# An index bound on the experts' gathers and additions, and the sort put first in the opening stage

## The chip, the cores and the metric

The kernel runs on one core of one Trainium2 chip. The metric is the device time of one execution in microseconds; the median of three runs is used. Lower is better.

## The reference

Four residual layers work on x, 2048 tokens (4 batches of 512) of 512 numbers each, all in float32:

1. Each token belongs, by its id, to one of four context matrices c (512 x 512), and takes tanh(g) times silu(h cᵀ) * (h cᵀ) times c, with h the layer-normalized token. In the kernel, "experts" of this stage are the four context matrices.
2. A gated feed-forward layer of width 2048, whose activations and weights are rounded to a small float format in blocks of 32.
3. Attention of eight heads over the channels, with queries from x and keys and values from the context.
4. A mixture of 64 experts (width 192, six per token, chosen in groups). An expert takes at most CAP = 96 tokens; further ones are dropped:

```
flat_e = topk_ids.reshape(-1)
order = argsort(flat_e);  se = flat_e[order]
pos = arange(Tn * K) - searchsorted(se, se, side='left')
valid = pos < CAP                      # CAP = 96
buf = zeros(E, CAP + 1, H).at[se, slot].set(x[tok])[:, :CAP]
h = silu(buf @ w_gate) * (buf @ w_up)
out = h @ w_down                       # weighted and added to each token's row
y + silu(x @ ws_gate) * (x @ ws_up) @ ws_down     # one shared expert for all tokens
```

Slots of an expert that no token takes are zero rows in `buf`, and their results are not used.

## The kernel before

The program is one pass over the four layers. In the first stage an order written out by hand fixes the instruction order on TensorE, ScalarE, VectorE and GpSimd (`tc.manual_schedule(engines={PE, ACT, DVE, POOL})`); SyncE's queue (SP), which issues most DMAs, is ordered by the scheduler. In the second and third layer the order is fixed on TensorE, ScalarE and VectorE, and in the expert stage by the scheduler alone.

The first stage does three things side by side.

- Sorting. Token ids become a one-hot table (`hot`, L341), TensorE counts ranks and totals (`rank_ps` L348, `tot_ps` L350), VectorE sums the totals over tiles (`scan`, L354 to L359), works out each token's place (`pos`, `place`, L374 to L387), writes one-hot rows (`hot_tile` L391, `hot_row` L399), TensorE inverts the table (`at_ps`, L406), and VectorE makes `to_row` (L423) and `from_row` (L425). With them GpSimd gathers sorted tiles of x by indirect DMA (`take`, L442), NS = 19 tiles of 128 rows, eleven of them ahead.
- The context. Four loads `c_sb` (L307, two buffers) are transposed by `turn_context(b)`: four chunks of four transposes (L294) and a copy by ScalarE (L295) into `cT`.
- The second layer's weights. `quantize()` rounds 24 blocks of weights on VectorE (L245 to L268), in pieces; `some_weights(us)` does pieces worth so many microseconds, so that they lie between the other work. A block's source is loaded by SP (L196, L213) into one of four buffers; when a block's `w_q` (L263) is made, `fetch_weights(1)` issues the next load. ScalarE makes `mx_wide` (L251) for each block, and `turn_weights` transposes the result.

For each sorted tile `sums_of` takes two passes on ScalarE (L150), `factors_from` works out the layer norm's factors for a group of tiles on VectorE (`ln_mean`, L156 and on), `normal` normalizes (L170), and the loop over i turns the tile, multiplies it by its context matrix twice (L474) with `squashed` and `gated` (L486) between, and adds the rows to the table `x_rows` in DRAM by an indirect DMA (L491).

Before the loop, SP also issues copies and zeros: x to `x_rows` (L311), zeros to the spare rows of `x_rows`, `h_rows` and `out` (L312 to L314), to all of `more_rows` (L316, L317), and the list of unused slots to `taken` (L318). `zeros` is a tile that VectorE clears at L298.

In the third stage the router fills `taken`: for every slot of every expert it notes which token sits there (`noted`, through `put`, L123). A slot that nobody takes keeps its number from `unused`, which points at one of the 96 spare rows T to T+95, rows of zeros in `h_rows` and rows that nobody reads in `out` and `more_rows`. At the end of this stage the last token tiles go through `groups_of`, `experts_of`, `counted` (L1041), `slots` and `noted` one after another.

In the expert stage `gather(e)` fetches 96 rows of 576 numbers (512 of the token, 64 weights) through column e of `idx` into `xg` (L1194, six buffers, six experts ahead); `turn` transposes them (`g_ps`, L1207), `hidden` multiplies by the gate and up weights (`gu_ps`, L1217), `finish` by the down weights (`e_y`, L1240), copies to `e_o` (L1242, four buffers) and adds the 96 rows to a table by an indirect DMA (L1243). Even experts add to `out`, odd ones to `more_rows`, the last three to `out`. Additions to one table follow each other. Weights of an expert come by three DMAs on SP (`e_gu`, `e_gu`, `e_dn`), up to 15 experts ahead. At the end `more_rows` is read back as `rest` (L1278), the shared expert's product (`sh_y`, L1294) is added to it (L1296) and the sum is added to `out` by GpSimd's DMAs (L1297).

Of the kernel before, what the change touches and what calls it, by code (L numbers as in the profile page):

```python
# [9 lines left out]
F32 = mybir.dt.float32  # L10
# [9 lines left out]
P = 128  # L20
B, S, D = 4, 512, 512
T = B * S
# [24 lines left out]
def flamingo_kernel(  # L47
# [19 lines left out]
    out: bass.AP,  # L67
):
    nc = tc.nc
    PE, ACT, DVE, POOL = (getattr(mybir.EngineType, e) for e in ("PE", "Activation", "DVE", "Pool"))  # L70
# [112 lines left out]
    with (  # L183
# [3 lines left out]
        tc.tile_pool(name="c_rows", bufs=2) as cp,  # L187
        tc.tile_pool(name="ps_t", bufs=4, space=PSUM) as ps_t,
        tc.tile_pool(name="ps_m", bufs=4, space=PSUM) as ps_m,
        tc.manual_schedule(engines={PE, ACT, DVE, POOL}),  # L190
    ):

        def rows_of(w, wT, rb):
# [81 lines left out]
        def some_weights(us):  # L275

            while us > 0:
                took = next(weights, None)
                if took is None:
                    return  # L280
                us -= took
# [3 lines left out]
                turn, q = rounded.popleft()  # L285
                turn(q)

        def turn_context(b):

            c_sb = c_rows.popleft()  # L290
            for k in range(KC):
                ps = ps_t.tile([P, D], F32, name="cT_ps", tag="t")
                for s in range(4):
                    nc.tensor.transpose(ps[:, bass.ts(s, P)], c_sb[:, s, bass.ts(k, P)], ident)  # L294
                nc.scalar.copy(cT[:, b * KC + k, :], ps)  # L295
# [5 lines left out]
        with tc.tile_pool(name="route0", bufs=1) as rp:  # L301

            fetch_weights(1)
            c_rows = deque()
            for b in range(B):
                c_sb = cp.tile([P, 4, D], F32, name="c_sb")
                nc.sync.dma_start(c_sb, cx[bass.ts(b, S), :].rearrange("(j p) d -> p j d", p=P))  # L307
                c_rows.append(c_sb)
                if b == 1:
                    fetch_weights(3)  # L310
            nc.sync.dma_start(x_rows[:T, :], x[:, :])  # L311
            nc.sync.dma_start(x_rows[T:, :], zeros[:, :D])  # L312
            nc.sync.dma_start(h_rows[T:TP, :], zeros[:CAP, :])
            nc.sync.dma_start(out[T:TP, :], zeros[:CAP, :D])  # L314
            for j in range(NT):
                nc.sync.dma_start(more_rows[bass.ts(j, P), :], zeros[:, :D])  # L316
            nc.sync.dma_start(more_rows[T:TP, :], zeros[:CAP, :D])  # L317
            taken_by = [nc.sync.dma_start(taken[1 : CAP * E + 1, :].rearrange("(s e) o -> s (e o)", e=E), unused)]  # L318

            th = keep.tile([P, 4], F32, name="th")  # L320
            nc.scalar.activation(th, gains[:, 0:4], AF.Tanh)
# [26 lines left out]
            nc.tensor.matmul(rank_ps.rearrange("p j e -> p (j e)"), before, hot2, start=True, stop=True)  # L348
            tot_ps = ps_m.tile([P, NT, NE0], F32, name="tot_ps", tag="m")
            nc.tensor.matmul(tot_ps.rearrange("p j e -> p (j e)"), ones, hot2, start=True, stop=True)  # L350
            turn_context(0)
            some_weights(2.5)
            scan = [rp.tile([P, NT, NE0], F32, name=f"scan{i}") for i in range(2)]
            nc.vector.tensor_copy(scan[0], tot_ps)  # L354
            cur, step = 0, 1
# [41 lines left out]
            for j in range(0, NT, 4):  # L397
# [2 lines left out]
                    hot_row[:, j : j + 4], column.unsqueeze(1).to_broadcast(wide),  # L400
                    row_i[:, j : j + 4].unsqueeze(2).to_broadcast(wide), ALU.is_equal,
                )
            turn_context(1)
            at_ps = ps_m.tile([P, 2, NS], F32, name="at_ps", tag="m")
            for j in range(NT):
                nc.tensor.matmul(at_ps, hot_row[:, j, :], hot_tile[:, :, j, :], start=j == 0, stop=j == NT - 1)  # L406

            own = rp.tile([1, NS], F32, name="own")
            own1 = rp.tile([1, NS], F32, name="own1")
# [30 lines left out]
        def take(i):  # L440
            xs = wp.tile([P, D], F32, name="xs", bufs=XS)
            nc.gpsimd.indirect_dma_start(  # L442
                out=xs[:, :],
                out_offset=None,
                in_=x[:, :],
                in_offset=bass.IndirectOffsetOnAxis(ap=from_row[:, i : i + 1], axis=0),
            )
# [67 lines left out]

        for i in range(XS):
            take(i)
        turn_context(2)
        some_weights(4.0)
        turn_context(3)  # L520
        sums_of(0)
        some_weights(4.0)
        factors_from(0)
        sums_of(1)
        sums_of(2)
        normal(0)
        some_weights(4.0)
        factors_from(1)
        for i in range(3, 5):
# [2 lines left out]
        for i in range(-2, NS):  # L532
            if i >= 0:
                turned(i, "s", "sT")
            if i + 2 < NS:
                turned(i + 2, "h", "hT")
            waiting = len(rounded)
            if waiting:
                turn_weights()
            if i >= 0:  # L540
                times_context(i, "sT", "y")
            if 0 <= i + 1 < NS:
                squashed(i + 1)
            some_weights(3.6)
            if 0 <= i + 1 < NS:
                gated(i + 1)
            if i + 2 < NS:
                times_context(i + 2, "hT", "z")
            if waiting > 1:
                turn_weights()  # L550
            if i + 3 < NS:
                normal(i + 3)
            if i >= 0:
                add_rows(i)
                if i + XS < NS:
                    take(i + XS)
            sums_of(i + 7)
            some_weights(3.6)
            factors_from(i + 4)
        while rounded or sources:  # L560
# [617 lines left out]
    with (  # L1178
# [10 lines left out]
        tables = out, more_rows  # L1189
        LAST = 3  # L1190
        gathered = {}
        def gather(e):
# [42 lines left out]
        def finish(e, aT):  # L1235

            _, dn, held = loaded.pop(e)
            y = ps_m.tile([CAP, D], F32, name="e_y", tag="m")
            for c in range(2):
                nc.tensor.matmul(y, aT[:, c, :], dn[:, c, :], start=c == 0, stop=c == 1)  # L1240
            o = xp.tile([CAP, D], F32, name="e_o", bufs=4)
            nc.scalar.copy(o, y)  # L1242
            nc.gpsimd.indirect_dma_start(  # L1243
                out=tables[e % 2 if e < E - LAST else 0][:, :],
                out_offset=bass.IndirectOffsetOnAxis(ap=idx[:, e : e + 1], axis=0),
                in_=o[:, :],
                in_offset=None,
                compute_op=ALU.add,
            )
# [5 lines left out]
        AHEAD = 6  # L1255
# [71 lines left out]
```

## Time and profile before

| what | us |
|---|---|
| median of 3 runs | 1227.52 (1226.75 to 1229.18) |
| the profiled execution's own time | 1232.19 |
| its span | 1230.4 |
| TensorE busy | 1018.0 (83%) |
| VectorE busy | 792.9 (64%) |
| ScalarE busy | 572.3 (47%) |
| GpSimd busy | 385.4 (31%) |

The profile is of one execution. Its page gives the busy time of each engine, the span in 40 slices, the DMA queues, the chain of work that ended last, and groups of instructions by source line. The timeline lists instructions by start and length, with the idle time before them and what ended it in brackets. Times count from the start of the span. TensorE's matmul is PE, its weight load PEld, VectorE is DVE, ScalarE ACT, GpSimd POOL, SyncE SP; a q behind a name is that engine's queue issuing a DMA. The stages lie at about 0 to 251 us (first layer), 251 to 528 (second), 528 to 866 (third, with the router) and 866 to 1182 (experts), and the rest is the end.

### The profile page before, as it was taken

The numbers are of one execution on the slowest core, as the hardware profiler recorded it, in microseconds if no ns is written. First come the engines' busy times: TensorE is split into PE (matmuls) and PEld (weight loads), VectorE is DVE, ScalarE is ACT, GpSimd is POOL, SyncE is SP. The second block draws the span as 40 slices with busy tenths as digits, with TensorE's granted clock in tenths as the row PEclk, the third lists the DMA queues.
The fourth block names the chain that finished last, engine by engine and source line by source line (L and its number), as shares of the span: only waits on it lengthen the run. The fifth ranks groups of instructions, "written<-read, shape, count | busy, mean of one in ns | idle before, by whom it ended". The sixth has DMA issues, their size and how long they took to land. (4 is left out here: it accounts for less than half of the span.)

```text
span 1230.4 us, 14849 instructions
## 1 busy us (share of the span) xinstructions
PE 1018.0 (83%) x4603; PEld 512.5 (42%) x4603; DVE 792.9 (64%) x1976; ACT 572.3 (47%) x1144; POOL 385.4 (31%) x526
## 2 busy tenths in 40 slices
PE   5488998627888888788999999971899999999994
PEld 4244444313333334344454444440455555544441
DVE  7699999948998999846888887862222222222221
ACT  3665765437676657584665666630111111111120
POOL 3122322200000000011544544554355435444424
PEclk8698999958999999999999999985899999999997
DMA  9834543331221111187121111027799999999978
GB/s 333 320 86 103 109 97 77 51 112 35 43 50 28 18 18 18 18 229 218 55 70 55 56 61 46 22 76 222 230 272 273 279 280 284 276 282 279 277 186 137
DMA packets 75806, 174.76 MB, mean 142 GB/s; under 512 B 13024, under 2 KB 14064, under 8 KB 75664
## 3 DMA queue, kind: packets, MB, share of 16 engines
q1 hardware_dynamic: 51696, 128.04, 34.4%
q0 software_dynamic: 23200, 45.16, 19.2%
q8 instruction: 38, 0.62, 0.2%
q10 hardware_dynamic: 832, 0.62, 0.2%
q14 instruction: 40, 0.33, 0.1%
HBM read 133.76 MB, written 44.20 MB: 145 GB/s over the span
## 5 line engine op out<-in xcount | busy, mean ns | idle before, releaser
L1217 PE MATMUL gu_ps<-e_gu,gT 128*96 128x384 f32 x512 | 178.3, 491 | 0.0
L1221 DVE SCALAR_TENSOR_TENSOR a<-s,xg,gu_ps 96x192 f32<-96x192 f32 x64 | 35.0, 546 | 149.7 <-ACT s L1219 145.1
L1240 PE MATMUL e_y<-e_dn,eaT 96*96 96x512 f32 x256 | 120.5, 592 | 0.1
L123 POOL DMA_INDIRECT taken<-token_no,to_i x96 | 97.1, 1012 | 51.1 <-issue 24.2
L1217 PEld LDWEIGHTS gu_ps<-e_gu,gT 128*96 128x96 f32 x512 | 79.2, 165 | 62.5 <-issue 62.2
L631 ACT ACTIVATE p<-at_s,low 128x512 f32<-128x512 f32 x128 | 87.7, 697 | 28.6 <-DVE low L622 27.1
L1242 ACT COPY e_o<-e_y 96x512 f32<-96x512 f32 x64 | 37.3, 582 | 134.4 <-PE e_y L1240 57.2
L622 DVE TENSOR_REDUCE low<-at_s 128x2 f32<-128x1024 f32 x64 | 77.7, 1215 | 34.1 <-PE at_s L617 34.1
L1209 DVE COPY gT<-g_ps 128x384 f32<-128x384 f32 x64 | 35.7, 558 | 97.9 <-PE g_ps L1207 91.5
L747 POOL DMA_DIRECT2D x_rows<-y_sb x15 | 12.9, 863 | 262.1 <-ACT y_sb L746 262.1
L718 PE MATMUL gu<-wgT,hT 128*128 128x512 bf16 x256 | 72.0, 407 | 20.7 <-DVE inter L731 13.5
L491 POOL DMA_INDIRECT x_rows<-y_sb,to_row x19 | 39.5, 2081 | 150.3 <-ACT y_sb L490 150.3
L718 PEld LDWEIGHTS <-hT 128*128 128x128 bf16 x512 | 50.1, 103 | 86.3 <-DVE inter L731 14.3
L1243 POOL DMA_INDIRECT out_dram<-e_o,idx x34 | 48.8, 1435 | 117.3 <-ACT e_o L1242 51.8
L891 ACT COPY pT<-p_ps 128x512 f32<-128x512 f32 x128 | 70.9, 600 | 31.2 <-PE p_ps L890 30.5
L1194 POOL DMA_INDIRECT xg<-h_rows,idx x64 | 60.0, 938 | 62.3 <-DVE a L1221 24.2
L890 PE MATMUL p_ps<-ident,p 128*128 128x128 f32 x512 | 73.3, 281 | 7.3 <-ACT hT L968 6.7
L890 PEld LDWEIGHTS p_ps<-ident,p 128*128 128x128 f32 x512 | 54.5, 141 | 58.3 <-issue 22.7
L474 PE MATMUL l_mm<-cT,sT 128*128 x152 | 75.1, 641 | 0.0
L1219 ACT ACTIVATE s<-gu_ps 96x192 f32<-96x192 f32 x64 | 21.0, 328 | 116.2 <-PE gu_ps L1217 109.8
L617 PE MATMUL at_s<-c_tile,q 64*128 64x512 f32 x256 | 72.0, 640 | 1.3 <-ACT p L631 1.3
L474 PE MATMUL l_mm<-cT,hT 128*128 x152 | 71.4, 614 | 1.9 <-ACT hT L461 1.9
(245 smaller groups left out, 2022.6 us busy)
## 6 DMA issues: line engine op xcount, KB each, us to landing
e_gu<-in_L_ffn_w_gate_dram SPq DMA_DIRECT2D x64, 384.0 KB
e_gu<-in_L_ffn_w_up_dram SPq DMA_DIRECT2D x64, 384.0 KB
e_dn<-in_L_ffn_w_down_dram SPq DMA_DIRECT2D x64, 384.0 KB
w_src<-in_L_ffn_w_gate_dram SPq DMA_DIRECT2D x8, 512.0 KB
c_sb<-in_ctx_dram SPq DMA_DIRECT2D x4, 1024.0 KB
w_src<-in_L_ffn_w_up_dram SPq DMA_DIRECT2D x8, 512.0 KB
more_rows<-zeros SPq DMA_DIRECT2D x16, 256.0 KB
w_src<-in_L_ffn_w_down_dram SPq DMA_DIRECT2D x8, 512.0 KB
```

Of the source, the lines that this page charges most:

```text
L123: ins = nc.gpsimd.indirect_dma_start(out=table[:, :], out_offset=bass.IndirectOffsetOnAxis(ap=to, axis=0), in_=what, in_offset=None)
L474: nc.tensor.matmul(ps.unsqueeze(1), aT[:, k, :], cT[:, bass.ds(at + k, 1), :], start=k == 0, stop=k == KC - 1)
L617: nc.tensor.matmul(s[:, h, :], t["q"][rows, bass.ts(i, P)], t["c"][rows, :], start=True, stop=True)
L622: nc.vector.tensor_reduce(low, tiles[j]["s", i], AX.X, ALU.max, negate=True)
L631: nc.scalar.activation(p[:, h, :], s[:, h, :], AF.Exp, bias=low[:, h : h + 1], accum_out=t["sums"][:, i, h : h + 1])
L718: nc.tensor.matmul(ps[:, i, :], hT[:, k, :], wT[:, k, bass.ts(c, 512)], start=k == 0, stop=k == KC - 1)
L890: nc.tensor.transpose(ps[:, k, :], p[:, h, bass.ts(k, P)], ident)
L891: nc.scalar.copy(tiles[j]["pT"][h][:, :, bass.ts(i, P)], ps)
L1194: nc.gpsimd.indirect_dma_start(out=g[:, :], out_offset=None, in_=h_rows[:, :], in_offset=bass.IndirectOffsetOnAxis(ap=idx[:, e : e + 1], a ...
L1217: nc.tensor.matmul(ps, gT[:, k, :], gu[:, :, k, :], start=k == 0, stop=k == KC - 1)
L1240: nc.tensor.matmul(y, aT[:, c, :], dn[:, c, :], start=c == 0, stop=c == 1)
L1243: nc.gpsimd.indirect_dma_start(out=tables[e % 2 if e < E - LAST else 0][:, :], out_offset=bass.IndirectOffsetOnAxis(ap=idx[:, e : e + 1], ...
```

## The change

There are three edits.

- In the expert stage, gathers and additions get `bounds_check=T - 1, oob_is_err=False`: an index above T-1, which is what an unused slot holds, is left out of the transfer. The rows of `xg` that a gather leaves out keep what was there, so each of the six buffers is cleared once by VectorE before its first gather. A skipped row's result is left out by the addition.
- In the first stage the piece of weight rounding that stood in the middle of the sort is gone, so VectorE does the sort first. `turn_context(0)` is split: two chunks ahead of the inverting matmuls (L406 before), two behind them; the turns of the other contexts move behind the gathers of x, with weight pieces and the first tile's sums, factors and normalization between them.
- SP's order is now written out too (SP joins the manual schedule). The x copy, the zeros and `taken` stand behind two weight pieces, so behind the load that the first block's `w_q` releases; the sixteen zeros of `more_rows` are spread over the loop's rounds. The fourth weight load stands behind the context loads.

```diff
-        tc.manual_schedule(engines={PE, ACT, DVE, POOL}),
+        tc.manual_schedule(engines={PE, ACT, DVE, POOL, SP}),
...
-        def turn_context(b):
-
-            c_sb = c_rows.popleft()
-            for k in range(KC):
+        def turn_context(b, chunks=range(KC)):
+
+            c_sb = c_rows[b]
+            for k in chunks:
...
                 if b == 1:
-                    fetch_weights(3)
-            nc.sync.dma_start(x_rows[:T, :], x[:, :])
-            nc.sync.dma_start(x_rows[T:, :], zeros[:, :D])
-            nc.sync.dma_start(h_rows[T:TP, :], zeros[:CAP, :])
-            nc.sync.dma_start(out[T:TP, :], zeros[:CAP, :D])
-            for j in range(NT):
-                nc.sync.dma_start(more_rows[bass.ts(j, P), :], zeros[:, :D])
-            nc.sync.dma_start(more_rows[T:TP, :], zeros[:CAP, :D])
-            taken_by = [nc.sync.dma_start(taken[1 : CAP * E + 1, :].rearrange("(s e) o -> s (e o)", e=E), unused)]
+                    fetch_weights(2)
+            fetch_weights(1)
...
-            turn_context(0)
-            some_weights(2.5)
+            turn_context(0, range(2))
...
-            turn_context(1)
             at_ps = ps_m.tile([P, 2, NS], F32, name="at_ps", tag="m")
             for j in range(NT):
                 nc.tensor.matmul(at_ps, hot_row[:, j, :], hot_tile[:, :, j, :], start=j == 0, stop=j == NT - 1)
+            turn_context(0, range(2, KC))
...
         for i in range(XS):
             take(i)
+        turn_context(1)
+        some_weights(4.0)
+        sums_of(0)
         turn_context(2)
+        factors_from(0)
+        normal(0)
         some_weights(4.0)
+
+
+        nc.sync.dma_start(x_rows[:T, :], x[:, :])
+        nc.sync.dma_start(x_rows[T:, :], zeros[:, :D])
+        nc.sync.dma_start(h_rows[T:TP, :], zeros[:CAP, :])
+        nc.sync.dma_start(out[T:TP, :], zeros[:CAP, :D])
+        nc.sync.dma_start(more_rows[T:TP, :], zeros[:CAP, :D])
+        taken_by = [nc.sync.dma_start(taken[1 : CAP * E + 1, :].rearrange("(s e) o -> s (e o)", e=E), unused)]
         turn_context(3)
-        sums_of(0)
-        some_weights(4.0)
-        factors_from(0)
         sums_of(1)
         sums_of(2)
-        normal(0)
         some_weights(4.0)
         factors_from(1)
...
             sums_of(i + 7)
+            if 0 <= i < NT:
+                nc.sync.dma_start(more_rows[bass.ts(i, P), :], zeros[:, :D])
             some_weights(3.6)
             factors_from(i + 4)
...
         def gather(e):
-            g = xp.tile([CAP, D + E], F32, name="xg", bufs=6)
+            g = xp.tile([CAP, D + E], F32, name="xg", bufs=AHEAD)
+            if e < AHEAD:
+                nc.vector.memset(g, 0.0)
             nc.gpsimd.indirect_dma_start(
                 out=g[:, :],
                 out_offset=None,
                 in_=h_rows[:, :],
                 in_offset=bass.IndirectOffsetOnAxis(ap=idx[:, e : e + 1], axis=0),
+                bounds_check=T - 1,
+                oob_is_err=False,
             )
...
                 in_=o[:, :],
                 in_offset=None,
+                bounds_check=T - 1,
+                oob_is_err=False,
                 compute_op=ALU.add,
             )
```

More of the change, by code (lines that the diff above doesn't have):

```diff
@@ L69, in flamingo_kernel @@
     nc = tc.nc
-    PE, ACT, DVE, POOL = (getattr(mybir.EngineType, e) for e in ("PE", "Activation", "DVE", "Pool"))
+    PE, ACT, DVE, POOL, SP = (getattr(mybir.EngineType, e) for e in ("PE", "Activation", "DVE", "Pool", "SP"))
     keep = ctx.enter_context(tc.tile_pool(name="keep", bufs=1))
@@ L303, in flamingo_kernel @@
             fetch_weights(1)
-            c_rows = deque()
+            c_rows = []
             for b in range(B):
@@ L1191, in flamingo_kernel @@
         gathered = {}
+        AHEAD = 6
         def gather(e):
-            g = xp.tile([CAP, D + E], F32, name="xg", bufs=6)
+            g = xp.tile([CAP, D + E], F32, name="xg", bufs=AHEAD)
+            if e < AHEAD:
+                nc.vector.memset(g, 0.0)
             nc.gpsimd.indirect_dma_start(
@@ L1252, in finish @@
                 load_expert(later, held)
-        AHEAD = 6
         for e in range(AHEAD):
```

## The prediction

> **What bounds the kernel now.** I read the page's slices first, then the windows by stage, then the timeline of the first 50 us, the chain of waits and GpSimd's timeline at the end.
>
> Windows by stage (columns: length, busy time of PE, PEld, DVE, ACT, POOL, granted clock, DMA share, GB/s):
>
> ```profile
> 0.00:251.00 251.00, 189.33 (x729) 102.55 (x730) 222.72 (x417) 143.33 (x260) 62.82 (x59) 0.89 0.53 146
> 20.00:40.00 20.00, 7.30 (x32) 6.56 (x32) 9.57 (x20) 7.11 (x13) 9.71 (x10) 0.50 1.01 362
> 866.00:1070.00 204.00, 203.21 (x754) 102.95 (x755) 57.66 (x126) 38.33 (x83) 92.39 (x79) 0.98 1.02 269
> 1070.00:1160.00 90.00, 86.48 (x323) 42.95 (x322) 24.20 (x54) 15.69 (x36) 42.04 (x36) 1.00 1.06 281
> 1202.00:1230.00 28.00, 11.14 (x32) 4.80 (x30) 5.02 (x7) 1.84 (x5) 13.81 (x16) 0.78 0.89 151
> ```
>
> The first stage (0 to 251) is VectorE's: 222.7 of 251 busy, and from 40 us on some 18.8 of every 20. Its hole is at 20 to 40, where VectorE works 9.57 us and the DMA engines are full. The expert stage is TensorE's, at 4.80 us an expert, with the DMA engines full as well; from 1070 on TensorE loses 3.5 us of 90. The last 28 us are the DMA engines'.
>
> The hole, from the timeline (start, duration; in brackets the idle time before and what ended it):
>
> ```profile
> 7.17 1.22 DVE L245 TENSOR_REDUCE mx_top<-w_src 128x32 f32<-128x1024 f32 x1 [2.53 <-DMA w_src<-in_L_ffn_w_gate_dram]
> 10.00 0.22 DVE L354 COPY scan<-tot_ps 128x64 f32<-128x64 f32 x1
> ...
> 17.68 0.62 SPq L311 DMA_DIRECT2D x_rows<-in_x_dram  x1
> 19.91 32.13 SPq L316 DMA_DIRECT2D more_rows<-zeros  x16
> 20.50 1.23 POOL L442 DMA_INDIRECT xs<-in_x_dram,from_row  x1 [16.80 <-DVE from_row L425]
> 37.56 0.72 ACT L150 ACTIVATE waste<-xs 128x512 f32<-128x512 f32 x1 [8.05 <-DMA xs<-in_x_dram,from_row]
> 39.25 0.17 DVE L156 TENSOR_SCALAR ln_mean<-ln_sums 128x2 f32<-128x2 f32 x1 [9.65 <-ACT waste L150]
> ```
>
> A block of weights stands before the sort and waits 2.53 us for its data. The first gather of x is issued at 20.50 and lands only at 37.5, because the copy of x and the zeros were queued ahead of it; VectorE waits 9.65 us for the sums of that tile.
>
> The experts' end, from the chain of waits (start, duration, what):
>
> ```profile
> 1093.52 0.57 ACT e_o L1242
> 1094.22 8.91 DMA out_dram<-e_o,idx
> 1103.20 0.59 ACT e_o L1242
> 1103.93 9.14 DMA out_dram<-e_o,idx
> ```
>
> and GpSimd's timeline:
>
> ```profile
> 1176.85 1.40 POOL L1243 DMA_INDIRECT out_dram<-e_o,idx  x1 [1.87 <-ACT e_o L1242]
> 1182.55 1.40 POOL L1243 DMA_INDIRECT out_dram<-e_o,idx  x1 [4.30 <-issue]
> 1190.84 1.40 POOL L1243 DMA_INDIRECT out_dram<-e_o,idx  x1 [6.88 <-ACT aT L1286]
> 1195.82 1.40 POOL L1243 DMA_INDIRECT out_dram<-e_o,idx  x1 [3.58 <-issue]
> 1201.75 11.55 POOL L1297 DMA_DIRECT2D out_dram<-rest  x13 [4.52 <-issue]
> ```
>
> From 1093 on, the additions to `out` follow each other every 9.7 to 10 us, one for two experts: 4.9 to 5.0 us an expert against TensorE's 4.80, so this chain binds and the gathers behind it in POOL's queue come late. TensorE ends the last expert at 1182.5, but the last addition is issued at 1195.82, and the 16 final writes (L1297) may only start behind it.
>
> **The change, part by part.** Sums are made against the profiled execution (span 1230.4, its time 1232.19); it stands 4.7 us above the median 1227.52, to which I carry the difference over.
>
> 1. Sort first. Without the block, the scan starts when `tot_ps` is there: the matmul ends at 5.18+0.63=5.81, the scan about 6.0 instead of 10.0. All of the sort moves by 4.0: from_row done at 16.2, first gather at 16.5. The block's first four steps (1.22+0.18+0.18+1.23, overlapped some 2.7) come later, so VectorE is ahead by 4.0-2.7=1.3. The matmuls of L406 now stand behind two chunks of the context's transposes instead of four; those wait for `c_sb` until 11.09 and end about 12.8, and the first `hot_row` is there at 12.3. No loss beyond a few tenths.
>
> 2. Copies and zeros behind the block. The x copy, the zeros of x_rows, h_rows, out and more_rows' pad and `taken` stand in SP's queue behind the fifth weight load, which waits for the first block's w_q: about 29 us. The sixteen more_rows zeros go between later weight loads. Gather 0 then meets only context and weight loads: 16.5+1.2 of issue+about 2 = 20. ScalarE gets to its sums only behind eight context copies (0.85 us apart, TensorE's third and fourth transposes of tile 0 from about 14.5, those of tile 1 to about 20.3, copies to 20.7), mx_wide (1.05) and two passes (1.65): 23.4. VectorE starts the block at 16.75, has 4.4 us of work before it needs the sums, and waits 2.4 us instead of 9.65. That makes 1.3+9.65-2.4=8.5, less the next wait.
>
> Late next: the context tiles 2 and 3. In SP's program order the load of tile 2 waits for all four chunks of tile 0 (16.5), that of tile 3 for tile 1 (20.3). ScalarE's order puts tile 3's copies ahead of the sums that VectorE wants at 36.0 (26.6 when the first factors end, plus 9.4 of block work). In the trace of before, tile 3 landed 7.6 us after its issue (17.6 to 25.2), which gives 28, transposes to 32, sums at 36: no wait. If it shares evenly with the gathers, 256 KB every 1.26 us, it lands at 30.5 and the wait is 2.7. I take 1.5 to 2: part gain 6.5. Bounds: 3 (context later still, and `gated(0)`, for which ScalarE is only some 2 us early, stalls) and 8.5.
>
> Here a rule speaks against the change. The row is 17 us from issue to use of gather 0. The Trainium skill, "DMA: Bandwidth & Descriptors", section "Queues, rings and completion order", says that each DMA engine takes turns between its queues packet by packet, so a gather would get about half the engines even behind a full SP queue: 256 KB at half of 362 GB/s is an estimated 1.5 us, landing about 24 and not 37.5. Then the wait would not be the copies' fault, and this part would give 1.3 instead of 6.5. The row decides: with the copy of x queued, turns were not equal shares. Among the context loads, whose rows are 2 KB like the gathers', I let the rule set the pessimistic end.
>
> Hidden: the x copy, issued at 29 to 30, takes at least the 11.9 us that SP waited for it, so about 45 with the gathers; the first addition to x_rows (L491, 73.5 before) comes about 65. The zeros are needed by the stages at 590 (`taken`) and 859 on. Weight loads run four blocks ahead of VectorE (34 us), which covers the copy now between them; uncovered, it would cost up to 12. From 251 to 866 I count nothing: every step keeps its order and shifts.
>
> 3. Six memsets of xg. They stand on VectorE between the small steps of groups_of for the tile before last (823.9 to 828). No row is 96x576; the 128x576 memset took 0.54, so 3.2 us. What waits for that chain is L1041 on TensorE, which starts at 832.06 behind first_layer's matmuls, while `chosen` was ready at 828.3: 3.8 us of cover, cost 0. The first memset also waits for old writes of x_tile rows (issued by 819.38); if it waited longer, everything in groups_of queues behind it. Bounds 0 to 3; below nothing no reason exists.
>
> 4. Index bound. By the reference's routing on its inputs, 4695 of 6144 slots are used; 1449 (23.6%) fall away, in 27 of 64 experts. POOL issues as many instructions as before (0.94 and 1.44 us). TensorE's 4.80 us an expert stay. What can go is the 3.5 us of late gathers and the lag at the end. An addition took 8.9 to 10.2 us under load; 23.6% of 9.1 is 2.1 us, which takes the chain from 9.8 to about 7.7 per two experts, well below 9.6. A second rule speaks against that: the same page's "Anatomy of one DMA — SWDGE (gpsimd) path" has about 2.0 us fixed and bytes/436 GB/s variable, so 196 KB is 0.45 us and dropping a quarter saves 0.1: the chain would still bind and this part be worth almost nothing. But the row's 9 us are far above that 2.45 estimate, hence mostly queueing, and the freed traffic (1449 rows of 2304 and of 2048 bytes, 6.3 MB, 22 us at 282 GB/s) shortens the queue itself. I take 3.3 of the 3.5.
>
> The end: expert 60 has 2 rows, 61 to 63 are full. Without lag (times of before less 3.5): 60 lands about 1171, e_o of 61 is ready at 1172.6, its addition lands 8.3 later as in the trace (1182.55 to 1190.84), those of 62 and 63 take 5 to 6 each: final writes start about 1192.5 instead of 1198.2. They are DMA-bound (28.6 us from 1201.75 to the span's end, while VectorE has the last sum at 1213.9), so the end moves with them: 5.7 to 7; I take 6. Bounds 0 and 8.
>
> Sum: 6.5+3.3+6=15.8. 1232.2-15.8=1216.4 in the profile, 1227.5-15.8=1211.7 as median, rounded 1212.
>
> **Rivals.**
> - Front only (0.15): skipped rows still occupy the DMA engines, or the fixed part rules. For it: the rule above. Against it: the queueing. 1227.5-6.5-(0 to 2)=1219 to 1221.
> - Experts only (0.13): gathers and context tiles crowd each other, and ScalarE's packed order stalls VectorE in the first rounds. 1227.5-9.3-(0 to 2)=1216 to 1218.
> - Slower (0.07): the bound makes POOL's indirect instructions dear. Place: POOL in the expert stage; per expert 0.94+1.44+2x0.30=2.98 of 4.80 now. It decides from 0.91 us more on each of the two; at twice their durations POOL needs 5.35, 64x0.55=35 more: 1227.5+35-6.5=1256. Against it: the gather of 128 rows takes 0.99, of 96 rows 0.94, 1.7 ns a row, and a comparison should be no more. For it: no row of before shows a bound.
> - Neither part works, within 2.5 us (0.03).
>
> **How the numbers follow.** Both parts work: 0.62, 1212, own range 1206 to 1217. Faster by over 0.2% (2.5 us, about what a measurement can tell): 0.62+0.15+0.13=0.90; same 0.03; slower 0.07. The range 1204 to 1221 takes in the first case with its bounds, experts only, and most of front only.
>
> **What would show it.** Right: scan at 6, first gather at 16.5, first ln_mean at about 24 instead of 39.25 with under 3 us of wait; VectorE's last block ending near 244 instead of 250.6; no wait of g_ps for xg after 1060; about 39 MB on the software queue (45.16 now, less 6.3); first L1297 some 13 us behind the last expert instead of 19. Wrong: POOL's L1243 or L1194 rows longer by 0.3 or more; ln_mean of tiles 1 and 2 waiting over 5 us on ScalarE; a first memset that waits.

## The result, and the profile after

The changed kernel takes 1215.43 us (median of 7 runs, 1211.99 to 1220.99); the kernel before took 1226.75 us beside it (7 runs, 1219.56 to 1231.46). The ratio is 0.9913, 95% interval 0.9884 to 0.9941: 7 to 14 us shorter, 10.7 by the ratio. The prediction had 15.8 us less, to 1212, with a range of 1204 to 1221. The profiled execution took 1220.99 us, its span is 1219.1, and 11.3 us shorter than the span of before.

The opening stage, from the timeline of the changed kernel (start, duration, engine, line, what; in brackets the idle time before and what ended it):

```profile
6.23 0.22 DVE L346 COPY scan<-tot_ps 128x64 f32<-128x64 f32 x1 [1.21 <-PE tot_ps L343]
16.74 1.23 POOL L434 DMA_INDIRECT xs<-in_x_dram,from_row  x1 [13.07 <-DVE factors L426]
22.72 0.72 ACT L150 ACTIVATE waste<-xs 128x512 f32<-128x512 f32 x1 [1.10 <-DMA xs<-in_x_dram,from_row]
24.41 0.17 DVE L156 TENSOR_SCALAR ln_mean<-ln_sums 128x2 f32<-128x2 f32 x1 [3.40 <-ACT waste L150]
30.25 0.62 SPq L519 DMA_DIRECT2D x_rows<-in_x_dram  x1
248.82 0.17 DVE L156 TENSOR_SCALAR ln_mean<-ln_sums 128x2 f32<-128x2 f32 x1 [6.41 <-DMA xt<-x_rows]
```

The scan starts at 6.2 (10.0 before), the first gather is issued at 16.7 (20.5) and used 6.0 us later (17.1), and VectorE waits 3.4 us for the first tile's sums (9.65). The last line starts the second stage. VectorE has finished its last weight piece when that wait begins: 248.82-6.41=242.4. In the timeline of before the same line stands at

```profile
256.29 0.17 DVE L156 TENSOR_SCALAR ln_mean<-ln_sums 128x2 f32<-128x2 f32 x1 [5.73 <-ACT waste L150]
```

so the first stage ended at 250.6 there. I call this instant the end of the first stage below.

The windows of the changed kernel by stage (columns as in the prediction):

```profile
0.00:251.00 251.00, 187.29 (x733) 103.79 (x733) 224.94 (x429) 146.24 (x266) 55.31 (x59) 0.90 0.56 154
20.00:40.00 20.00, 7.34 (x45) 6.79 (x44) 15.29 (x45) 15.16 (x31) 8.19 (x9) 0.76 1.12 412
866.00:1070.00 204.00, 203.85 (x764) 102.95 (x763) 57.99 (x127) 39.13 (x85) 95.32 (x79) 1.00 1.02 260
1070.00:1160.00 90.00, 89.43 (x339) 45.03 (x337) 25.43 (x56) 16.52 (x37) 44.94 (x37) 1.00 0.99 257
```

VectorE works 15.3 of the 20 us in which it worked 9.6, and TensorE 89.4 of the 90 us from 1070 in which it worked 86.5. Yet the chain of waits still has additions of 9 us, one behind the other:

```profile
1078.19 9.35 DMA out_dram<-e_o,idx
...
1088.34 8.89 DMA out_dram<-e_o,idx
```

The software queue's line on the page, first of before, then of the changed kernel (packets, MB, share of 16 engines):

```profile
q0 software_dynamic: 23200, 45.16, 19.2%
```

```profile
q0 software_dynamic: 23200, 38.87, 17.0%
```

The bytes fell by 6.29 MB, close to 1449 x (2304+2048), which is 6.31, so the bound leaves out the rows that it should. The number of packets is the same, only more of them are small: those under 512 bytes rose from 13024 to 15194 on the page. With the additions' bound alone (adds_bound, below) they rise by 1449, one for each left-out row; with the gathers' alone by 721, about one for two rows.

The end, GpSimd's and VectorE's timelines:

```profile
1178.68 1.40 POOL L1253 DMA_INDIRECT out_dram<-e_o,idx  x1 [7.34 <-ACT aT L1297]
1184.45 1.40 POOL L1253 DMA_INDIRECT out_dram<-e_o,idx  x1 [4.37 <-ACT aT L1297]
1190.25 9.75 POOL L1308 DMA_DIRECT2D out_dram<-rest  x11 [4.39 <-DVE rest L1307]
...
1205.81 0.85 POOL L1308 DMA_DIRECT2D out_dram<-rest  x1 [0.44 <-DVE rest L1307]
1204.64 0.75 DVE L1307 SCALAR_TENSOR_TENSOR rest<-sh_y,factors,rest 128x512 f32<-128x512 f32 x1 [0.96 <-PE sh_y L1305]
```

TensorE ends the last expert at 1174.0 (1182.5 before). The final writes begin 16.2 us behind it (19.2 before), and the last of them is issued 0.4 us after VectorE's last sum. Before, VectorE's last sum was there at 1213.9 and the last write was issued at 1217.1. From the issue of the first final write to the end of the span it is 28.9 us, and it was 28.7 before.

The difference of the two profiled executions, cut at five instants:

| from, to | before | after | difference |
|---|---|---|---|
| start, end of the first stage | 250.6 | 242.4 | -8.2 |
| to the issue of the last `taken` entry (L123) | 598.2 | 599.0 | +0.8 |
| to the issue of the first expert gather | 10.3 | 13.8 | +3.5 |
| to TensorE's end of the last expert | 323.5 | 318.8 | -4.7 |
| to the end of the span | 47.9 | 45.1 | -2.8 |

The sum is -11.3 us before rounding. The +3.5 was not foreseen: the last entry of the list was issued at 841.40, and the list was reloaded only at 850.99, 9.6 us later (6.2 before).

### The profile page after: what moved, and what is told of

Read it like the earlier page. It is cut to its first block, busy times and chain, and to the rows that moved or that the text cites. A ratio compares the mean times of both kernels' runs of the same rounds, so it can differ in the third digit from the quotient of the medians.

```text
span 1219.1 us, 14968 instructions
## 1 busy us (share of the span) xinstructions
PE 1011.7 (83%) x4581; PEld 512.9 (42%) x4603; DVE 795.7 (65%) x1982; ACT 570.9 (47%) x1144; POOL 379.4 (31%) x526
## 2 busy tenths in 40 slices
DMA packets 75807, 168.48 MB, mean 138 GB/s; under 512 B 15194, under 2 KB 16234, under 8 KB 75664
## 3 DMA queue, kind: packets, MB, share of 16 engines
q0 software_dynamic: 23200, 38.87, 17.0%
## 4 chain that ended last, share of the span: by engine, by line
PE 33%; DMA 8%; DVE 8%; ACT 3%; issue 2%; POOL 1%; SPq 0%; POOLq 0%; DVEq 0%; ACTq 0%
PE gu_ps L1227 10%; PE e_y L1250 7%; DMA out_dram<-e_o,idx 5%; PE first_ps L978 3%; PE at_o L926 3%; DVE low L625 3%; PE at_s L620 2%; PE sh_y L1305 2%; ACT p L634 2%; PE p_ps L893 2%; DMA taken<-token_no,to_i 1%; PE g_ps L1217 1%; PE over_ps L907 1%; DVE hw L960 1%; POOL taken L123 1%
## 5 line engine op out<-in xcount | busy, mean ns | idle before, releaser
L123 POOL DMA_INDIRECT taken<-token_no,to_i x96 | 96.6, 1007 | 48.5 <-issue 23.8
L625 DVE TENSOR_REDUCE low<-at_s 128x2 f32<-128x1024 f32 x64 | 77.8, 1216 | 38.6 <-PE at_s L620 38.2
L1202 POOL DMA_INDIRECT xg<-h_rows,idx x64 | 63.0, 984 | 64.8 <-DVE a L1231 28.5
L483 POOL DMA_INDIRECT x_rows<-y_sb,to_row x19 | 30.8, 1619 | 153.1 <-ACT y_sb L482 153.1
## 6 DMA issues: line engine op xcount, KB each, us to landing
e_dn<-in_L_ffn_w_down_dram SPq DMA_DIRECT2D x64, 384.0 KB, 14.8
```

The costliest lines, as they stand in the source:

```text
L123: ins = nc.gpsimd.indirect_dma_start(out=table[:, :], out_offset=bass.IndirectOffsetOnAxis(ap=to, axis=0), in_=what, in_offset=None)
L625: nc.vector.tensor_reduce(low, tiles[j]["s", i], AX.X, ALU.max, negate=True)
L1202: nc.gpsimd.indirect_dma_start(out=g[:, :], out_offset=None, in_=h_rows[:, :], in_offset=bass.IndirectOffsetOnAxis(ap=idx[:, e : e + 1], a ...
```

## The experiments

Ratios are to the kernel before, run in turn on the same chip; each has its 95% interval.

**Are front and experts two gains?** One kernel takes only the first stage's edits, one only the bound:

```diff
 front_only = changed kernel
-                bounds_check=T - 1,
-                oob_is_err=False,
-            if e < AHEAD:
-                nc.vector.memset(g, 0.0)
 bound_only = kernel before, with these lines added
```

> The changed kernel without the index bound and without the six memsets: only the new order of the first stage. My theory (the front and the experts are two separate gains that add up): VectorE's last operation of the first stage ends near 242.4 us rather than 250.6, the first expert gather is issued 4 to 7 us earlier than before, the experts keep their stalls for late gathers (3.5 us), and the whole is 6 to 8 us shorter than before, ratio 0.994 to 0.995. Rival (the head start is given back behind the first stage, and the gain seen is the bound's): under 3 us shorter. Side question: in the changed kernel the last list entry took 9.5 us from its issue to the list's reload where before took 6.2; if that is the price of the earlier stage it is near 9.5 here too, if it is chance it may be either.

> The kernel before with only the index bound on gathers and additions and the six memsets; the first stage as before. My theory: VectorE's memsets cost nothing, PE's wait for late gathers falls from 3.5 to about 0.5 us, the last expert ends 3 to 4 us earlier against the first gather, and the first final write comes about 16 us behind the last expert rather than 19; together 4 to 7 us shorter than before, ratio 0.994 to 0.997. Rival (the whole gain is the front's): within 1.5 us of before.

front_only: 0.9956 (0.9937 to 0.9976), 5.4 us shorter, a little under what was expected; its first stage ends at 243.2. bound_only: 0.9946 (0.9925 to 0.9968), 6.6 us. The product is 0.9902 beside the changed kernel's 0.9913, so within the intervals the two add up. In bound_only's profile the last expert ends 318.7 us behind the first gather (323.5 before), the first final write comes 13.9 us behind that expert, and the span ends 41.9 us behind it (47.9 before). The step from the last list entry to the reload took 4.8 us in front_only and 7.4 in bound_only, and 5.2 to 7.2 in every later kernel of this study. The changed kernel's 9.6 is the longest of all, and front_only shows that it is not the price of the earlier stage. From the last entry to the first gather, the eight profiles with the gathers' bound and its memsets have 10.7 to 13.8 us (mean 11.7), the six without them 9.2 to 11.4 (mean 10.1). No run separates the memsets from the bound, so the cause of these 1.5 us is open.

**Which half of the bound?**

```diff
 gathers_bound = changed kernel; in finish(e):
-                bounds_check=T - 1,
-                oob_is_err=False,
 adds_bound = changed kernel; in gather(e): the same two lines and the memset taken out
```

> The changed kernel with the bound on the gathers alone; the additions write their spare rows again. Theory A (a left-out row still takes its turn as a small packet, so the additions' bound is worth little): the same as the changed kernel within 1.5 us, the software queue's bytes about 3 MB above it. Theory B (the additions' chains on the two tables are what the bound relieves, as my prediction had it): PE's late gathers stay near 0.5 us, but the tail is back to 19 us from the last expert to the first final write, and the whole is 3 us or more slower than the changed kernel.

> The changed kernel with the bound on the additions alone; the gathers fetch spare rows again and the six memsets are gone. Theory A (late gathers are mended by fewer gathered bytes): PE's wait for late gathers is back to about 3.5 us and the whole 2 to 4 us slower than the changed kernel. Theory B (gathers wait behind the additions in the one software queue, so the additions' bound mends them): the wait stays under 1 us and the time is that of the changed kernel within 1 us.

gathers_bound: 0.9917 (0.9888 to 0.9947), the changed kernel's time. adds_bound: 0.9966 (0.9944 to 0.9988), the time of front_only, which has no bound at all. So the additions' bound is worth nothing that these runs can see, and the gathers' bound with its memsets is the whole gain. Theory A's number for late gathers failed: adds_bound's profile has 0.2 us of that wait, not 3.5. The wait is not steady. front_only's profile, without any bound, has none, but 2.8 us of waiting for `e_gu`. What is steady is the length of the stage. From the first gather to the end of the last expert, the six profiles without a bound on the gathers have 319.8 to 323.5 us, the eight with one 317.7 to 318.8. The additions follow each other every 9.84 to 9.97 us per two experts without it (experts 2 to 60), and every 9.59 to 9.74 with it; TensorE's own pace is 2 x 4.80=9.6.

**What sets the 9 us of an addition?** One kernel leaves out nearly all the added rows (its output lacks most of the experts' part), one stops the weight loads, so that later experts use the weights of earlier ones:

```diff
 adds_none, in finish(e):
-                bounds_check=T - 1,
+                bounds_check=0,
 no_weights, in finish(e):
-                load_expert(later, held)
+                loaded[later] = gu, dn, held
```

> The changed kernel with the additions' bound at row 0, so that all their rows but row 0 are left out (the output lacks the experts' part); gathers and everything else as in the changed kernel. Theory A (a left-out row is still one small packet, and an addition's time is its turns among the other queues' packets): the software queue keeps its 23200 packets, the bytes of the additions (about 9.6 MB of those that were left) go, and an addition still lands 7.5 to 9 us after its issue, the total within 3 us of the changed kernel. Theory B (what the prediction used: an addition's time goes with its written rows): it lands in 3 to 5 us, a table's additions no longer queue up, and the first final write comes about 10 us behind the last expert rather than 16.

> The changed kernel without the experts' weight loads behind the fifteenth expert: expert e uses the weights that its tile held before (the output of these experts differs). Theory A (the 9 us of an addition and the 8.6 us of a gather are waiting among the weights' packets): both fall to 4 to 5.5 us once the loads have stopped, and PE's pace of 9.7 us per two experts becomes the only bound; the total is 2 to 6 us shorter than the changed kernel, the tail included. Theory B (the addition's time is its own: fixed cost and the read and write of the table's rows): it stays within 1.5 us of 9.

Landing times from 870 to 1160, the DMA view of the changed kernel, then adds_none, then no_weights (last number: median us from issue to landing):

```profile
xg<-h_rows,idx POOLq DMA_INDIRECT x58, 8.6
out_dram<-e_o,idx POOLq DMA_INDIRECT x29, 9.0
```

```profile
xg<-h_rows,idx POOLq DMA_INDIRECT x58, 8.7
out_dram<-e_o,idx POOLq DMA_INDIRECT x30, 8.9
```

```profile
xg<-h_rows,idx POOLq DMA_INDIRECT x56, 3.3
out_dram<-e_o,idx POOLq DMA_INDIRECT x31, 4.1
```

An addition that writes next to nothing takes 8.9 us; one with its rows, but no weight packets beside it, takes 4.1. Beside the weights the time is spent among their packets and has little to do with the rows: front_only, which leaves out none, has 8.9 as well. At the end, where no weights load, the rows do count: the last two additions land in 2.5 us in adds_none and in 4.1 in gathers_bound. The queue kept its 23200 packets in adds_none, with 29.30 MB. The totals are 0.9884 (0.9851 to 0.9918) for adds_none and 0.9891 (0.9808 to 0.9974) for no_weights; both intervals overlap the changed kernel's.

At the end adds_none did what theory B said: the first final write comes 9.9 us behind the last expert instead of 16. GpSimd's first and VectorE's last line of adds_none, and the landing of its final writes behind that of the changed kernel (DMA view, 1170 to 1215):

```profile
1182.15 5.32 POOL L1308 DMA_DIRECT2D out_dram<-rest  x6 [2.84 <-issue]
1202.89 0.75 DVE L1307 SCALAR_TENSOR_TENSOR rest<-sh_y,factors,rest 128x512 f32<-128x512 f32 x1 [0.96 <-PE sh_y L1305]
```

```profile
out_dram<-rest POOLq DMA_DIRECT2D x16, 256.0 KB, 9.7
```

```profile
out_dram<-rest POOLq DMA_DIRECT2D x16, 256.0 KB, 6.7
```

VectorE's last sum, at 1203.6, stands 31.4 us behind the last expert (1172.3); in the changed kernel and in before it is 31.4 as well, since the sixteen sums wait for `sh_y` (in adds_none each of them), nearly all 1.94 us apart. The last write is issued right behind that sum in both kernels, but this is not the end. In the changed kernel the last write still takes 9.7 us to land, behind the writes queued ahead of it; in adds_none it takes 4.9, and the span ends 40.2 us behind the last expert instead of 45.1.

So the end follows the first final write. From its issue to the end of the span, thirteen of the fourteen profiles of this study have 28.0 to 28.9 us, whether the write comes 13.7 us behind the last expert or 22.1. Only in adds_none is it more, 30.3: there the writes wait for VectorE's sums.

**Which half of the first stage?**

```diff
 sort_only = front_only; x copy, zeros and `taken` issued right behind
 the context loads, as before, and the zeros of more_rows with them
 copies_only = kernel before; the same lines moved behind
         turn_context(2)
         some_weights(4.0)
+        nc.sync.dma_start(x_rows[:T, :], x[:, :])
...
         turn_context(3)
```

> The kernel before with the sort's chain first in VectorE's order and the context's turns as in the changed kernel, but copies and zeros issued at their old place; no index bound. My step 1: scan near 6 us, the first gather issued at 16.5 rather than 20.5, but its rows still behind the copies, so that VectorE's last operation of the first stage ends only 0.5 to 2 us earlier than before (250.6), at 248.5 to 250. Rival (the early sort is what counts, the copies hardly matter): it ends 5 us or more earlier, at 245.5 or under.

> The kernel before with only the copies and zeros moved to where the changed kernel has them; the sort's order as before and no index bound. My step 2: the first gather is issued at 20.5 as before but lands some 10 us sooner, VectorE's wait for the first tile's sums falls from 9.65 to under 4 us, and the last operation of the first stage ends 5 to 7 us earlier than before, near 244 to 245.5. Rival: the weight loads issued around it keep the gathers just as late, and it ends at 248.5 or later.

The rival was right about the sort; copies_only ended between what was expected and what its rival said. sort_only: 0.9941 (0.9916 to 0.9967); copies_only: 1.0003 (0.9971 to 1.0034). The first stage of sort_only ends at 242.3, as early as the changed kernel's. Its SyncE, GpSimd and VectorE timelines:

```profile
16.68 3.54 SPq L307 DMA_DIRECT2D c_sb<-in_ctx_dram  x2
20.82 0.62 SPq L312 DMA_DIRECT2D x_rows<-in_x_dram  x1
16.75 1.23 POOL L442 DMA_INDIRECT xs<-in_x_dram,from_row  x1 [13.08 <-DVE factors L434]
24.29 0.17 DVE L156 TENSOR_SCALAR ln_mean<-ln_sums 128x2 f32<-128x2 f32 x1 [3.26 <-ACT waste L150]
```

Here the x copy stands at its old place in the program, and still it moved. SP issues in the order of its timeline: the load of context tile 2 in front of it waits for tile 0's buffer, and with the context's turns behind the sort that buffer comes free at 16.7 instead of 14.8. The copy goes out at 20.8 instead of 17.7, and the first gather 4.07 us ahead of it instead of 2.82 us behind it. Copies_only on the other hand, from ScalarE's and VectorE's timelines:

```profile
43.17 0.72 ACT L150 ACTIVATE waste<-xs 128x512 f32<-128x512 f32 x1 [9.82 <-DMA xs<-in_x_dram,from_row]
59.54 0.69 DVE L478 TENSOR_TENSOR s<-s,l_mm 128x512 f32<-128x512 f32 x1 [5.63 <-ACT s L473]
253.69 0.17 DVE L156 TENSOR_SCALAR ln_mean<-ln_sums 128x2 f32<-128x2 f32 x1 [5.71 <-DMA xt<-x_rows]
```

The wait for the first sums is gone, but the copy, issued at 25.2, now meets the later gathers (issued from 20.5, one every 1.3 us): the sums of a later tile wait 9.8 us, and VectorE waits 5.6 for `s` and 1.8 for `mx_wide`. The stage ends at 248.0: 2.6 us won of 9.65, too little for the timing to tell from nothing. Neither kernel is a pure case: in both, SP's order is the written one, and sort_only also has the context's turns and the weight pieces in their new places.

**Why does the copy hold the gathers up?** The DMA view of before, 24 to 28 us and then 28 to 32 us (packets, MB, share of 16 engines):

```profile
q1 hardware_dynamic: 38, 1.98, 132.5%
q0 software_dynamic: 16, 0.07, 4.5%
```

```profile
q1 hardware_dynamic: 17, 1.11, 84.5%
q0 software_dynamic: 17, 0.07, 5.2%
```

In the second window both queues move 17 packets, in the first SP's moves more than twice as many. SP's are of 65 KB on average in the second, the gathers' of 4 KB. The copy of x was therefore cut into halves of columns:

```diff
 copy_pieces = kernel before
-            nc.sync.dma_start(x_rows[:T, :], x[:, :])
+            for half in range(2):
+                cols = bass.ts(half, D // 2)
+                nc.sync.dma_start(x_rows[:T, cols], x[:, cols])
```

> The kernel before, its order and its index lists untouched, with the copy of x cut into two column halves, so that its packets are of 1 KB rather than up to 64 KB. In the traces so far the software queue moved 16 packets in 4 us while the copy ran, and the copy's queue 17 to 38: equal turns, unequal packets. Theory A (turns by packet): the first gather, issued at 20.5 as before, lands near 26 to 29 rather than 37.5, VectorE's wait for the first sums falls from 9.65 to under 3 us, and the first stage ends 2 to 6 us earlier than 250.6. Theory B (what was issued first goes first): the gather lands at 36 or later whatever the packets, and the stage ends at 250 or later, as the copy itself gets no faster.

0.9926 (0.9903 to 0.9950), 9 us shorter (6 to 12), with three lines. The same two windows of copy_pieces, then VectorE's timeline:

```profile
q1 hardware_dynamic: 937, 0.96, 68.2%
q0 software_dynamic: 186, 0.63, 38.7%
```

```profile
q0 software_dynamic: 231, 0.76, 53.7%
q1 hardware_dynamic: 640, 0.65, 48.3%
```

```profile
29.48 0.17 DVE L156 TENSOR_SCALAR ln_mean<-ln_sums 128x2 f32<-128x2 f32 x1
246.72 0.17 DVE L156 TENSOR_SCALAR ln_mean<-ln_sums 128x2 f32<-128x2 f32 x1 [6.10 <-ACT waste L150]
```

The gathers have half of the engines' time instead of 5%, VectorE does not wait for the first sums at all, and the stage ends at 240.6, earlier than in the changed kernel. The counts are not one for one with small packets (937 to 186, 640 to 231), so what exactly the engines take turns by is open. The copy itself still runs beside the gathers in these windows, in packets of 1 KB. One thing more differs: the cut copy holds SP up, so that the zeros of `more_rows` are issued from 38.6 us instead of 19.9. No run separates the two, so part of the relief may come from the later zeros.

**The parts that paid.** First without the moved copies and the additions' bound; then the expert stage with smaller weight packets:

```diff
 sort_gathers = sort_only, with gather(e) of the changed kernel
 weights_halved = changed kernel, in load_expert:
-        nc.sync.dma_start(gu[:, 0, :, :], e_gate[e].rearrange("(p k) f -> p k f", k=KC))
-        nc.sync.dma_start(gu[:, 1, :, :], e_up[e].rearrange("(p k) f -> p k f", k=KC))
+        for part, w in enumerate((e_gate[e], e_up[e])):
+            w = w.rearrange("(p k) f -> p k f", k=KC)
+            for k in range(0, KC, 2):
+                nc.sync.dma_start(gu[:, part, k : k + 2, :], w[:, k : k + 2, :])
-        nc.sync.dma_start(dn, e_down[e].rearrange("(p c) d -> p c d", c=2))
+        for c in range(2):
+            nc.sync.dma_start(dn[:, c, :], e_down[e].rearrange("(p c) d -> p c d", c=2)[:, c, :])
```

> The sort first, copies and zeros at their old place, and the bound on the gathers alone: the parts that paid in the runs so far. If the parts add up, 7 + 5 us shorter than before, ratio 0.990 to 0.992, the same as the changed kernel (0.9913) within its interval: then the moved copies and the additions' bound are worth nothing. If the changed kernel needs them, it is 3 us or more slower than the changed kernel, ratio over 0.994.

> The changed kernel with each expert's weight loads cut in two, so that the packets that additions and gathers wait among are half as large (1.5 and 2 KB rather than 3 and 4). Theory A (turns by packet): an addition lands in 6 to 7.5 us rather than 9, a gather in 5.5 to 7 rather than 8.6, the weights later, the total 1 to 4 us shorter than the changed kernel unless the weights come too late. Theory B (the total bytes in the queues set the wait): an addition stays at 8.5 to 9.5 us.

sort_gathers: 0.9890 (0.9849 to 0.9932), no slower than the changed kernel. weights_halved: 0.9867 (0.9817 to 0.9917), which overlaps the changed kernel's interval. From its DMA view, 870 to 1160:

```profile
xg<-h_rows,idx POOLq DMA_INDIRECT x56, 6.9
more_rows<-e_o,idx POOLq DMA_INDIRECT x30, 7.5
out_dram<-e_o,idx POOLq DMA_INDIRECT x30, 7.9
```

A gather fell by 1.7 us, an addition by 1.1 to 1.5: less than theory A's 1.5 to 3 for the additions, more than theory B allows. The additions now keep TensorE's pace exactly, 9.59 us for two experts.

Last, all that paid in one kernel: copy in halves, weights in halves, the gathers' bound; sort, place of the copies and additions as before.

> The parts that paid, in one kernel: the kernel before with the copy of x in two column halves (1 KB packets), the experts' weight loads cut in two, and the index bound on the gathers alone with its six memsets; the sort's order and the place of copies and zeros as before, the additions unbounded. If the gains add up: copy in halves 0.9926 and halved weights with the bound 0.9867/0.9956 = 0.991, so about 0.984 of before, 4 to 10 us shorter than the changed kernel; VectorE's last operation of the first stage ends near 240.6, an addition lands in 7 to 8 us. If the two reliefs are one (the same time is saved once, and the stage behind takes it back): 0.987 to 0.992, no better than the changed kernel with halved weights.

0.9870 (0.9829 to 0.9910), median 1210.3 us: 5 us under the changed kernel's 1215.4 of another session, with intervals that overlap. The first stage ends at 241.1 and additions land in 7.5 to 7.6 us, as expected. By the ratio it is 16 us shorter than before; whether the parts add up in full (0.984) or not quite (0.987), its interval does not decide.

## Why the prediction was right, and where it was not

- **Sum and side.** Both parts work, as front_only and bound_only show, and the kernel is faster. The range holds, but it took in "experts only" and most of "front only" as well. The forecast gain of 15.8 us was 10.7 by the ratio, the front's 6.5 was 5.4, the bound's 9.3 was 6.6.
- **First stage, 6.5 us: right in sum, wrong in its split.** The stage ended 8.2 us earlier in the trace, and the timed front_only gained 5.4. Step 1 gave the sort 1.3 and step 2 the copies the rest. The runs show the stage ending 8.3 us earlier in sort_only and 2.6 us earlier in copies_only, whose time is that of before (1.0003, 0.9971 to 1.0034). What failed: step 2 saw that the load of context tile 2 waits for tile 0's turns (16.5 in the prediction, 16.7 in the trace), but not that the x copy stands behind that load in SP's queue. With the sort first the gather gets ahead of the copy without the copy being moved, and that is why the sum held. Its lateness of the context, 1.5 to 2 us, did not show: `ln_mean` of tiles 1 and 2 came at 36.45 without a wait.
- **The rule that was set aside.** The Trainium skill, "DMA: Bandwidth & Descriptors", section "Queues, rings and completion order", says that an engine takes turns between queues by packets. The prediction turned this into half the bytes, found 24 us where the row had 37.5, and concluded that turns were not equal. The step from packets to bytes was the error: where the row had 17 packets of each queue, they were of 65 and 4 KB. With the copy in small packets (copy_pieces) the first gather is used at 27.4, and so a cheap cure was passed over. Equal turns themselves show in one of the four windows only.
- **Memsets, 0 us: right up to the list's last entry.** It was issued 7.4 us earlier, nearly all of the first stage's 8.2. Whether the memsets have a part in the 1.5 us between that entry and the first gather is open.
- **Late gathers, 3.3 us: the size is right, the cause is not.** TensorE's wait for `xg` fell by 3.0 and the stage by 4.7 in this pair, by 3.5 between the means of the six profiles without the gathers' bound and of the eight with it. But the step let an addition shrink by 2.1 us with its rows, and it took 9.0 us with 23.6% of the rows left out and 8.9 with nearly all left out. The objection drawn from the second rule, the same page's "Anatomy of one DMA — SWDGE (gpsimd) path", that leaving a quarter of the rows out saves almost nothing, held on that point; the estimate of 2.45 us for the whole addition is short of the 4.1 without weight traffic. "Mostly queueing" was right too (no_weights). That the additions' bound helps was wrong; the gathers' bound does, by adds_bound and gathers_bound. Why 3.3 MB less in gathers helps, and 3.0 MB less in additions does not, is not settled here.
- **The end, 6 us: the path is right, the lead of the first write was taken too large.** The step moved the end with the first final write because the writes behind it are DMA-bound, and so it was: 28.7 us from the first write to the end before, 28.9 after. VectorE's last sum, 31.4 us behind the last expert, does not hold the end until the first write comes as early as in adds_none. But the first write was foreseen some 13 us behind the last expert and came at 16.2, so the end gained 2.8. The addition of expert 61 was issued 4.1 us ahead of the last expert's end, where the step had 6.4 (1179.0 less 1172.6), and from it to the first write it was 20.3 us, not 19.9. One profile does not fix this term: bound_only has the first write at 13.9 and an end 6.0 us shorter, and over the profiles with the gathers' bound and the additions' rows (seven, the first write at 13.7 to 16.7) the end is 43.3 us in the mean, against 48.7 in the six without the bound.
- **Rivals.** "Front only" named the right fact (a skipped row still takes its turn), which decides for the additions alone. "Slower", by dear GpSimd instructions, did not happen: a gather took 0.98 us instead of 0.94, an addition 1.43 instead of 1.44.

In short: 8.2 for 6.5, 4.7 for 3.3, 2.8 for 6, and 4.3 lost between the stages that no step had. That the three come to 15.7 beside the 15.8 of the forecast is luck. Of the 4.3, 3.5 lie behind the last list entry in this pair of executions, 1.5 in the mean over the profiles; why the rest of the forecast gain does not show in the time is not settled.

## What to carry to other kernels

Before moving a transfer out of another's way, look at the packet sizes of the two queues in the window where they meet: cutting a contiguous DRAM-to-DRAM copy into rows of 1 KB gave 9 us here, and halving weight packets shortened gathers and additions by 1.1 to 1.7 us each. Leaving rows out of an indirect DMA saves bytes but not packets, so ask whether the wait is made of bytes or of turns. And where writes queue up at the end, look at when the last of them lands, not at when it is issued: here the last issue stood close behind VectorE's last sum, and still the end moved with the first write.

## What the runs showed of the hardware that was not expected

- A left-out row stays in the queue as a packet: 23200 packets with the bound, without it, and with nearly all added rows left out. A left-out row of an addition is one packet under 512 bytes: 1449 more of them with 1449 rows left out (adds_bound).
- The sixteen final writes take 28.0 to 28.9 us from the first issue to the end of the span, in every profile but the one where they wait for VectorE (30.3).
- A contiguous copy from DRAM to DRAM goes out in packets of 65 KB, and beside them the software queue had 5% of the engines' time.
- From the end of the first stage to the last list entry, where the kernels hardly differ, the profiles have 592 to 600 us (592.2 in copies_only, 599.0 in the changed kernel, 599.6 in sort_gathers). One pair of profiles can't carry a difference of a few us across that stretch: stages have to be compared each on its own, over several profiles, or by the timed ratios.
